# Attention block with a routed feed-forward on one core: the query projections of two heads over two halves of the rows, in seven products of summed blocks

## The chip, the cores and the metric

The kernel runs on one core of one Trainium2 chip. The metric is the device time of one launch in microseconds (us); less is better. A launch has five engines with a queue of their own each: TensorE (PE in the profile, and PEld for the loads of its stationary operand), VectorE (DVE), ScalarE (ACT), GpSimd (POOL) and SyncE (SP, which here only issues transfers). PSUM, into which TensorE writes, has eight banks of 512 numbers for each of its 128 partitions.

## What is computed

There are 8 sequences of 512 rows of 256 numbers, all in f32. The reference, cut to its core:

```python
def attn(x):                                   # b, t = 8, 512; 4 groups of 4 query heads, head size 128
    q = (x @ wq + bq).reshape(b, t, 4, 4, 128).transpose(0, 2, 3, 1, 4)
    k, v = halves of (x @ wkv + bkv) per group  # one key and one value head for each group
    q, k = q + pe, k + pe                      # pe: sinusoidal positions
    scores = where(causal, einsum("bgqtd,bgksd->bgqts", q, k) / sqrt(128), -inf)
    out = einsum("bgqts,bgksd->btgqd", softmax(scores), v)
    return out.reshape(b, t, 2048) @ wo

def ffn(h):                                    # 64 experts, 6 for each row, at most 64 rows for each expert
    probs = softmax(h @ gate_w.T); w, idx = top_k(probs, 6)
    y = sum over the 6 of w * down(silu(gate(h)) * up(h))    # rows beyond an expert's 64 are dropped
    return y + (silu(h @ sh_gate.T) * (h @ sh_up.T)) @ sh_down.T

x = x + layernorm(attn(layernorm(x)))
x = x + layernorm(ffn(layernorm(x)))
```

The change touches only `x @ wq + bq + pe`, for 22 of the 32 pairs of a sequence and a group of four query heads.

## The kernel before

The order of the work on every engine is written out by hand: inside `tc.manual_schedule` each engine runs its instructions in the order in which the code issues them. A main loop goes over 128 steps `k`. A step belongs to sequence `b = k // 16`, to place `s = k % 16` in it, to group `g = s // 4` and to part `m = k % 4` of the causal triangle; it handles four blocks of 32 rows for the four heads of its group. A step issues, in this order:

- `scores(k, q)` for q = 3, 2, 1, 0 (L404): one product of the 128 stacked queries with up to 512 keys into a bank of the pool `ps_s` (three banks). DVE then adds the mask and takes the minimum (L408, called the reduce here), and ACT takes the exponential and the row sum (L412). Between the first two and the last two of these, `turned(k - 1)` transposes the weights of the step before in blocks of 32 on DVE (L440), SP writes them to memory in four transfers to `ex_d` (L444) and reads them back as `et` (L450).
- `weigh(k)`: DVE takes the reciprocal of the sums (L418), and POOL multiplies the four blocks by it (L422, four instructions).
- `projections(k)` (L500): mostly four products of an attention output with `wo_sb` into the pool `ps_o`.
- `queries(k + 2)` (L360): the queries of two heads for one half of the rows of a sequence. The four blocks of 128 rows of a sequence, 0 to 3, make two halves, the inner one (1, 2) and the outer one (0, 3). The 256 numbers of a row lie in two chunks `c` of 128, so this is four products of 256 columns each, two chunks times two heads, into one bank; DVE then adds bias and positions, once for each head (L365, into tiles tagged `qt`).
- `mix(k - 2)` (L475): five products of values with `et` into `pav`; ACT adds the value bias (L486).
- `group_step(k)`: for m = 1 the keys of the next group (`keys`, L311, evicted by DVE at L313), for m = 2 and 3 half of its values (`values`, L322, evicted by ACT).

`pq` (queries), `pav`, `pk`, `pv` and most other results share the pool `ps_m` of three banks, used in turn. Pools `ps_s`, `ps_m` and `ps_o` fill all eight banks.

Between these parts `side(s, place)` issues the feed-forward of the sequence before (norms, the shared expert `shared`, the routing `route`, which ends in long chains on DVE), `ahead` prepares the next sequence (from s = 6: load, norm statistics on DVE at L80, `rs_a` on POOL at L90, normalising on DVE at L109, then at s = 9 and 10 the transposed rows `xnt`), and from step 94 on `routed` runs the 64 experts in 32 pairs, whose weights are loaded to tiles tagged `wgu` and `wd`. In the shared expert the gate product `psg` and the up product `psu` (L865) both lie in `ps_m` until DVE has combined them (L878, L879).

Of the kernel before, what the change touches and what calls it, by code (L numbers as in the profile page):

```python
# [11 lines left out]
F32 = mybir.dt.float32  # L12
# [28 lines left out]
ET_ROWS = EARLY * T  # L41
LROW = ROW + NX

@with_exitstack
def sandwich_kernel(ctx, tc, x, wq, bq_t, wkv, bk_t, bv, wo, gate_wt, w_gate, w_up, w_down,
# [7 lines left out]
    ps_s = ctx.enter_context(tc.tile_pool(name="ps_s", bufs=3, space=PSUM))  # L53
    ps_m = ctx.enter_context(tc.tile_pool(name="ps_m", bufs=3, space=PSUM))
    ps_o = ctx.enter_context(tc.tile_pool(name="ps_o", bufs=1, space=PSUM))
# [10 lines left out]
    lxg_d = dram.tile([NT - ET_ROWS, LROW], F32, tag="lxg_d", name="lxg_d")  # L66
    ly_d = dram.tile([NT - ET_ROWS, E], F32, tag="ly_d", name="ly_d")

    ident = const.tile([P, P], F32, tag="ident", name="ident")
# [78 lines left out]
    with ExitStack() as part:  # L148
# [158 lines left out]
        def keys(b, g):  # L307
            s = seqs[b]
            pk = ps_m.tile([P, T], F32, tag="m", name=f"pk_{b}_{g}")
            for c in range(NC):  # L310
                nc.tensor.matmul(pk, lhsT=wkv_sb[:, c, g, 0, :], rhs=s["xnt"][:, c, :], start=c == 0, stop=c == NC - 1)  # L311
            kt = s["kt"][g] = p2.tile([D, T], F32, tag="kt", name=f"kt_{b}_{g}")
            nc.vector.scalar_tensor_tensor(kt, pk, bk_sb[:, g : g + 1], pe_sb, ALU.add, ALU.add)  # L313

        def values(b, g, n):
            s = seqs[b]
            if n == 0:
                s["v"][g] = p2.tile([P, NI, D], F32, tag="v", name=f"v_{b}_{g}")
            pv = ps_m.tile([P, 2, D], F32, tag="m", name=f"pv_{b}_{g}_{n}")
            for i in range(2):  # L320
                for c in range(NC):
                    nc.tensor.matmul(pv[:, i, :], lhsT=s["xnt"][:, c, ts(2 * n + i, P)], rhs=wkv_sb[:, c, g, 1, :],  # L322
                                     start=c == 0, stop=c == NC - 1, skip_group_check=True)
            on_act(s["v"][g][:, ts(n, 2), :], pv)
# [24 lines left out]
        def queries(k):  # L349

            half, pair = divmod(k, 2)
            b, n = divmod(half, 2 * G)
            g, inner = divmod(n, 2)
            cols = slice(1, 3) if inner else slice(0, NI, 3)
            if not pair:
                halves[half] = p2.tile([D, 2 * NI, QPG, BS], F32, tag="qt", name=f"qt_{half}")
            pq = ps_m.tile([P, 2, 2, P], F32, tag="m", name=f"pq_{k}")
            for n in range(2):
                for c in range(NC):
                    nc.tensor.matmul(pq[:, n, :, :], lhsT=wq_sb[g][:, c, ts(2 * pair + n, D)],  # L360
                                     rhs=seqs[b]["xnt"][:, c, :].rearrange("p (u v) -> p u v", v=P)[:, cols, :],
                                     start=c == 0, stop=c == NC - 1, skip_group_check=True)
            for n in range(2):
                h = 2 * pair + n
                nc.vector.scalar_tensor_tensor(  # L365
                    halves[half][:, :, h, :].rearrange("d (u r) t -> d u r t", u=2),
                    pq[:, n, :, :].rearrange("d u (r t) -> d u r t", t=BS), bq_sb[:, g * QPG + h : g * QPG + h + 1],
                    pe_sb.rearrange("d (u r t) -> d u r t", u=NI, t=BS)[:, cols, :, :], ALU.add, ALU.add)

        by_rows = {}  # L370
# [97 lines left out]
        def mix(k):  # L468
            b, g, m, _ = units_of(k)
            et = live.pop(k)["et"]  # L470

            pav = ps_m.tile([P, QPG, 2, HALF], F32, tag="m", name=f"pav_{k}")
            for n, _, first, count in placed(k):
                for j in range(count):
                    nc.tensor.matmul(pav[:, :, n % 2, :], lhsT=seqs[b]["v"][g][:, j, :], rhs=et[:, :, first + j, :],  # L475
                                     start=j == 0, stop=j == count - 1, skip_group_check=True)
            if k % 2 == 0:
                results[k // 2] = {i: p2.tile([D, QPG, P], F32, tag="ao", name=f"ao_{k}_{i}", bufs=3)
                                   for i in tiles_at(k // 2)}
            bias = bv_sb[:, g : g + 1]  # L480
            for n, _, _, _ in placed(k):
                ao = results[k // 2][n // 2][:, :, ts(n % 2, HALF)]
                if k == NK - 1 and n < NI:
                    nc.vector.tensor_scalar_add(ao, pav[:, :, n % 2, :], bias)  # L484
                else:
                    nc.scalar.activation(ao, pav[:, :, n % 2, :], AF.Identity, bias=bias)  # L486
# [45 lines left out]
        def route(b, xg, l):  # L532

            lg = l.pop("lg")
            pg = ps_m.tile([P, NI, NX], F32, tag="m", name=f"pg_{b}")
            for i in range(NI):
# [25 lines left out]
            if b >= EARLY:  # L562

                yield
                pp = ps_m.tile([P, NI + 1, NX], F32, tag="m", name=f"pp_{b}")
                for i in range(NI + 1):
# [17 lines left out]

            pc = ps_m.tile([P, 2, P], F32, tag="m", name=f"pc_{b}")
            for j in range(NI):
# [12 lines left out]
        def tables():  # L599


            pm = ps_m.tile([NX, CAP], F32, tag="m", name="pm")
            nc.tensor.matmul(pm, lhsT=ident[:, NX:], rhs=keyed[0][:, :CAP], start=True, stop=True)
# [5 lines left out]
            for n, _ in enumerate(best(first, both)):  # L609
                if n % 2:  # L610
                    yield
            pk = ps_m.tile([P, NM], F32, tag="m", name="pslot")
            cols = ident[:NX, :NX].rearrange("p (m k) -> p k m", k=2)
# [12 lines left out]
        def free_slots():  # L626
# [10 lines left out]
            yield  # L637
            pf = ps_m.tile([P, 2, NX], F32, tag="m", name="pfree")
            nc.tensor.matmul(pf[:, 0, :], lhsT=onesf, rhs=both[:, CAP:], start=True, stop=True)
# [59 lines left out]
        def gate_up(key):  # L699
            l = pairs[key]  # L700
            pgu = ps_m.tile([P, 2, F], F32, tag="m", name=f"pgu_{key}")
            for c in range(2):
# [7 lines left out]
        def gate_up_hidden(key):  # L710
            l = pairs[key]
            pgu = l.pop("pgu")
            nc.vector.scalar_tensor_tensor(l["hid"], l["hid"], 1.0, pgu[:, 0, :], ALU.add, ALU.mult)
            nc.vector.scalar_tensor_tensor(l["hid"], l["hid"], 0.5, pgu[:, 1, :], ALU.mult, ALU.mult)
# [10 lines left out]
        def down(key):  # L725
            l = pairs[key]
            pd = ps_m.tile([P, E], F32, tag="m", name=f"pd_{key}")
            for c in range(2):
# [105 lines left out]

        def shared(b, xt2, l, banks="mmmmmm"):

            hid = p1.tile([P, len(SH_CHUNKS), T], F32, tag="hid", name=f"hid_{b}")
            banks, todo = iter(banks), {}

# [18 lines left out]
            for n, (f0, fw) in reversed(list(enumerate(SH_CHUNKS))):  # L858
                mw = min(P, fw + NX // 2)
                pgu = []  # L860
                for w_sb, name in ((sg_sb, "psg"), (su_sb, "psu")):
                    tag = next(banks)
                    pp = {"m": ps_m, "s": ps_s}[tag].tile([P, T], F32, tag=tag, name=f"{name}_{b}_{n}")
                    for c in range(NC):
# [11 lines left out]

                def hidden(n=n, fw=fw, gs=gs, pgu=pgu):
                    nc.vector.scalar_tensor_tensor(gs[:fw, :], gs[:fw, :], 1.0, pgu[0][:fw, :], ALU.add, ALU.mult)  # L878
# [17 lines left out]
            for n in range(2):  # L896
                py = ps_m.tile([P, 2, E], F32, tag="m", name=f"py_{b}_{n}")
                for k in range(2):
# [10 lines left out]
        def feed_forward(b):  # L909
# [50 lines left out]
            def shared_gate():  # L960
                l["f"] = shared(b, l["xt2"], l, "mmmmss" if b == B - 2 else "mmmmmm")
                next(l["f"])
# [183 lines left out]
        for k in range(NK):  # L1146
# [14 lines left out]
            scores(k, 1)  # L1161
            scores(k, 0)
            if k == NK - 1:
                projections(k)
# [4 lines left out]
            side(s, "A")  # L1169
            if k < NK - 1:  # L1170
                projections(k)
# [3 lines left out]
            if s == 9 and b <= EARLY + 1:  # L1175
                next(ahead)()
            if k + 2 < NK:
                queries(k + 2)
            if finishing:
                next(routed, None)  # L1180
            side(s, "M")
            if k >= 2:
                mix(k - 2)
            if b <= EARLY and s == 8:
                next(ahead)()
            if active and not finishing:
                next(routed, None)
            for _ in range((1, 1, 1, 1, 1, 1, 0, 0, 0, 0, 0, 0, 2, 2, 2, 2, 2, 2, 2, 1, 1, 1, 1)[k] if k < NH + 7 else 0):
                next(zeroing, None)
            if k == FIRST_FREE:  # L1190

# [36 lines left out]
        with tc.For_i(0, table["rest"], 1) as n:  # L1228
# [21 lines left out]
            for b in range(EARLY, B - 1):  # L1250
                y = p2.tile([P, NI, E], F32, tag="xnt", name=f"rest_y_{b}")
                nc.sync.dma_start(out=y, in_=rows_of(ly_d, b * T - ET_ROWS))
                for i in range(NI):
                    py = ps_m.tile([P, E], F32, tag="m", name=f"rest_py_{b}_{i}")
                    nc.tensor.matmul(py, lhsT=gts[b - EARLY][:, ts(i, P)], rhs=pairs["late"]["dd"], start=True, stop=True)
# [56 lines left out]
```

## Time and profile before

| | |
|---|---|
| time, median of 3 runs | 1380.87 us (1380.31 to 1383.84) |
| the profiled execution's own time | 1379.57 us |
| its span on the core | 1377.9 us |
| granted clock of TensorE | 0.997 |
| busy: PE / DVE / ACT / POOL | 1351.6 / 812.9 / 544.5 / 430.5 us |
| instructions on PE / DVE | 6354 / 2695 |

The profile is of one execution. "L360 PE MATMUL pq<-xnt,wq_sb 128x256" is a group of instructions: the line of the kernel, the engine, the operation, output<-inputs by tile name, and the shape of the output. An f32 product shows as two MATMUL instructions. Durations of neighbouring matmuls overlap in the record, so the time that a group takes on PE is read from where it starts to where the next group starts. In the timeline each line gives start, length, engine, line and tiles, and in brackets the idle time of that engine just before, with what released it.

### The profile page before, as it was taken

Reading aid. Unit: us, or ns where it says so; the run is one execution under the profiler, and the core shown is the slowest. Engines: PE = TensorE matmul, PEld = TensorE weight load, DVE = VectorE, ACT = ScalarE, POOL = GpSimd, SP = SyncE. Lnnn points to the kernel's source line nnn. Section 1 sums busy time; section 2 is a strip of 40 time slices with the busy share of each in tenths; the row PEclk is TensorE's granted clock in tenths of the full one; section 3 lists DMA queues with packets and bytes.
Section 4 is the critical chain, followed back from the end, with each engine's and each line's share of the span. In section 5 each row is a group of like instructions: output and inputs, shape, how many; then the busy total and the mean of one; then the engine's idle time right before and its main releaser. Section 6 shows DMA issues by size and latency. Waiting matters only on the chain. (4 is left out here: it accounts for less than half of the span.)

```text
span 1377.9 us, 20286 instructions
## 1 busy us (share of the span) xinstructions
PE 1351.6 (98%) x6354; PEld 1032.8 (75%) x6354; DVE 812.9 (59%) x2695; ACT 544.5 (40%) x1655; POOL 430.5 (31%) x732
## 2 busy tenths in 40 slices
PE   8999999999999999999999999999999999999997
PEld 6778887788778887788778876777666676777774
DVE  5565466655675466555765557566655545567555
ACT  3333344334443343334433443333443334435433
POOL 3222231213221232123221232124544454446521
PEclk9999999999999999999999999999999999999999
DMA  7666666555664566455664565459998889687712
GB/s 253 185 184 185 184 184 199 162 146 157 203 182 128 149 204 182 146 156 162 199 184 130 148 188 162 127 170 279 304 277 250 242 239 303 181 247 232 250 51 70
DMA packets 167386, 261.30 MB, mean 190 GB/s; under 512 B 17756, under 2 KB 141629, under 8 KB 167277
## 3 DMA queue, kind: packets, MB, share of 16 engines
q1 hardware_dynamic: 129389, 207.29, 50.8%
q10 hardware_dynamic: 31744, 43.26, 10.0%
q0 software_dynamic: 6144, 9.44, 3.4%
q8 instruction: 51, 0.84, 0.3%
q14 instruction: 58, 0.48, 0.1%
HBM read 147.99 MB, written 111.94 MB: 189 GB/s over the span
## 5 line engine op out<-in xcount | busy, mean ns | idle before, releaser
L422 POOL TENSOR_SCALAR e<-e,recip 128x512 f32<-128x512 f32 (+1 forms) x504 | 243.6, 521 | 727.0 <-DVE recip L418 632.7
L412 ACT ACTIVATE e<-e,least 128x32 f32<-128x32 f32 (+1 forms) x504 | 258.6, 514 | 257.4 <-DVE least L408 243.2
L475 PE MATMUL pav<-et,v 128*128 128x256 f32 x1280 | 298.3, 380 | 4.9 <-DMA et<-ex_d 4.8
L404 PE MATMUL psc<-kt,qt 128*128 128x32 f32 (+15 forms) x1024 | 277.3, 409 | 4.2 <-DVE least L408 3.1
L486 ACT ACTIVATE ao<-pav,bv_sb 128x256 f32<-128x256 f32 x255 | 107.2, 471 | 424.8 <-PE pav L475 404.1
L475 PEld LDWEIGHTS pav<-et,v 128*128 128x128 f32 x1280 | 242.9, 190 | 41.0 <-DMA et<-ex_d 4.9
L408 DVE CUSTOM_DVE_ANT_0 e<-psc,mask 128x32 f32<-128x32 f32 (+1 forms) x504 | 203.4, 429 | 102.1 <-PE psc L404 99.8
L500 PE MATMUL po<-wo_sb,ao 128*128 128x256 f32 x1024 | 242.2, 381 | 1.1 <-DVE ao L484 1.1
L360 PE MATMUL pq<-xnt,wq_sb 128*128 128x256 f32 x1024 | 242.0, 379 | 0.0
L500 PEld LDWEIGHTS po<-wo_sb,ao 128*128 128x128 f32 x1024 | 193.1, 190 | 57.8 <-issue 21.2
L360 PEld LDWEIGHTS pq<-xnt,wq_sb 128*128 128x128 f32 x1024 | 193.1, 190 | 27.6 <-issue 1.3
L404 PEld LDWEIGHTS psc<-kt,qt 128*128 128x128 f32 x1024 | 161.3, 191 | 65.3 <-DVE least L408 31.5
L440 DVE STREAM_TRANSPOSE eb<-e 128x1024 f32<-128x1024 f32 (+1 forms) x252 | 197.4, 821 | 1.9 <-POOL shift_y L806 1.1
L365 DVE SCALAR_TENSOR_TENSOR qt<-pq,bq_sb,pe_sb 128x256 f32<-128x256 f32 x256 | 111.4, 476 | 134.5 <-PE pq L360 134.5
L412 ACT ACTIVATION_READ_ACCUMULATOR e<-e,least 128x1 f32 x504 | 94.6, 188 | 0.0
L418 DVE RECIPROCAL recip<-total 128x4 f32<-128x4 f32 x128 | 22.8, 178 | 114.4 <-ACT e L412 113.0
L741 POOL DMA_INDIRECT y_d<-dd,idx x32 | 51.0, 1594 | 82.8 <-DMA y_d<-dd,idx 33.9
L322 PEld LDWEIGHTS pv<-wkv_sb,xnt 128*128 128x128 f32 x512 | 66.4, 192 | 4.2 <-issue 1.5
L322 PE MATMUL pv<-wkv_sb,xnt 128*128 128x128 f32 x512 | 67.7, 275 | 0.0
L311 PE MATMUL pk<-xnt,wkv_sb 128*128 128x512 f32 x128 | 61.2, 601 | 0.0
L313 DVE SCALAR_TENSOR_TENSOR kt<-pk,bk_sb,pe_sb 128x512 f32<-128x512 f32 x32 | 24.0, 750 | 56.8 <-PE pk L311 56.8
L115 DVE COPY ht<-pth 88x256 f32<-88x256 f32 x32 | 13.4, 418 | 64.2 <-PE pth L721 64.1
(212 smaller groups left out, 1119.5 us busy)
## 6 DMA issues: line engine op xcount, KB each, us to landing
ex_d<-eb SPq DMA_DIRECT2D x504, 160.0 KB
et<-ex_d SPq DMA_DIRECT2D x126, 640.0 KB
wgu<-in_w_gate ACTq DMA_DIRECT2D x32, 352.0 KB
wgu<-in_w_up ACTq DMA_DIRECT2D x32, 352.0 KB
wd<-in_w_down ACTq DMA_DIRECT2D x32, 352.0 KB
y<-y_d ACTq DMA_DIRECT2D x10, 512.0 KB
x<-in_x SPq DMA_DIRECT2D x7, 512.0 KB
out_dram<-x SPq DMA_DIRECT2D x7, 512.0 KB
```

The lines of the kernel that those rows point to most:

```text
L311: nc.tensor.matmul(pk, lhsT=wkv_sb[:, c, g, 0, :], rhs=s["xnt"][:, c, :], start=c == 0, stop=c == NC - 1)
L322: nc.tensor.matmul(pv[:, i, :], lhsT=s["xnt"][:, c, ts(2 * n + i, P)], rhs=wkv_sb[:, c, g, 1, :], start=c == 0, stop=c == NC - 1, skip_gro ...
L360: nc.tensor.matmul(pq[:, n, :, :], lhsT=wq_sb[g][:, c, ts(2 * pair + n, D)], rhs=seqs[b]["xnt"][:, c, :].rearrange("p (u v) -> p u v", v=P ...
L365: nc.vector.scalar_tensor_tensor(halves[half][:, :, h, :].rearrange("d (u r) t -> d u r t", u=2), pq[:, n, :, :].rearrange("d u (r t) -> d ...
L404: nc.tensor.matmul(psc[:, :w], lhsT=halves[k // 2][:, at, :, :].rearrange("d h t -> d (h t)"), rhs=seqs[b]["kt"][g][:, :w], start=True, st ...
L408: nc.vector.tensor_tensor_reduce(out=e, in0=psc[:, :w].rearrange("p (c t) -> p c t", t=BS), in1=mask[:, T - w :].rearrange("p (c t) -> p c ...
L412: nc.scalar.activation(e, e, AF.Exp, bias=l["least"][:, q : q + 1], scale=-1.0, accum_out=l["total"][:, q : q + 1])
L422: engine.tensor_scalar(e, e, recip[:, q : q + 1], 1.0, ALU.mult, ALU.mult)
L440: nc.vector.transpose(eb[:, :, first : first + count, :, :].rearrange("p a j r t -> p j a r t"), weighed[k % 2][:, end - count : end, :, : ...
L475: nc.tensor.matmul(pav[:, :, n % 2, :], lhsT=seqs[b]["v"][g][:, j, :], rhs=et[:, :, first + j, :], start=j == 0, stop=j == count - 1, skip ...
L486: nc.scalar.activation(ao, pav[:, :, n % 2, :], AF.Identity, bias=bias)
L500: nc.tensor.matmul(po[b][i // 2][:, i % 2, :], lhsT=ao[:, h, :], rhs=wo_sb[:, n // 2 * QPG + h, :], start=n == 0 and h == 0, stop=n // 2 = ...
```

## The change

For the groups 2 to 23 of the launch (counted over sequences: group index `4 * b + g`), the queries of two heads over both halves of the rows are formed together. Before, they are eight products of 128x128 weights with 256 columns of `xnt`: two heads, two halves, two chunks. Seen as a 2x2 block matrix of weights (head by chunk) times a 2x2 block matrix of rows (chunk by half), they are now seven products of blocks and of sums of blocks, in the form of Strassen's scheme with shared sums. The sums of weights (`join_heads`, once for each of the four groups) and of rows (`join_rows`, once for each of six sequences) are made on POOL. The seven products and the sums of their results are spread over three steps: `ask` and `ask_sum` in an even step, `answer`, `ask_rest` and `ask_fourth` in the next step, `answer_fourth` after the scores of the one after that. Groups 0, 1 and 24 to 31 keep `queries`.

One bank moves from `ps_m` (now two) to a new pool `ps_b`, which holds the products 4 to 7 (`back`); after the last such group the function `bank` hands it out in turn with the other two. The third product takes a bank of `ps_s`. In the shared expert of the first five sequences `psu` takes banks of `ps_s` instead of `ps_m`. In most even steps (`quiet`) `projections` and `ask` are issued before `weigh` instead of after it. The temporary tiles lie where the experts' tiles lie later.

```diff
+TH = T // 2
+JOINED_FROM, JOINED_TO = 2, (EARLY + 1) * G
-    ps_m = ctx.enter_context(tc.tile_pool(name="ps_m", bufs=3, space=PSUM))
+    ps_m = ctx.enter_context(tc.tile_pool(name="ps_m", bufs=2, space=PSUM))
+    ps_b = ctx.enter_context(tc.tile_pool(name="ps_b", bufs=1, space=PSUM))
+    banks = {"late": False, "kept": 0, "since": 0}
+    def bank(shape, name, kept=False):
+        banks["since"] += 1
+        if banks["late"] and not kept and banks["since"] > 2 - banks["kept"]:
+            banks["since"] = 0
+            return ps_b.tile(shape, F32, tag="b", name=name)
+        banks["kept"] += kept
+        return ps_m.tile(shape, F32, tag="m", name=name)
...
+        def join_heads(g):
+            t = p3.tile([P, 4, 2, D], F32, tag="wgu" if g >= 2 else "wd", name=f"heads_{g}")
+            w = wq_sb[g].rearrange("p c (n k d) -> p c k n d", k=2, d=D)
+            nc.gpsimd.tensor_add(t[:, 0], w[:, 0, 1], w[:, 1, 1])
+            nc.gpsimd.tensor_sub(t[:, 1], t[:, 0], w[:, 0, 0])
+            nc.gpsimd.tensor_sub(t[:, 2], w[:, 0, 0], w[:, 0, 1])
+            nc.gpsimd.tensor_sub(t[:, 3], w[:, 1, 0], t[:, 1])
+            joined[g] = t
+        def join_rows(b):
+            (x11, x12), (x21, x22) = [sides_of(seqs[b]["xnt"], c) for c in range(NC)]
...
+            nc.gpsimd.tensor_sub(t[:, 0], x12, x11)
+            nc.gpsimd.tensor_sub(t[:, 1], x22, t[:, 0])
+            nc.gpsimd.tensor_sub(t[:, 2], x22, x12)
+            nc.gpsimd.tensor_sub(t[:, 3], x21, t[:, 1])
+        def ask(k):
...
+            f = {1: (w[:, 0, 0, pair], x11), 2: (w[:, 1, 0, pair], x21), 3: (j[:, 3, pair], x22),
+                 4: (w[:, 1, 1, pair], t[:, 3]), 5: (j[:, 0, pair], t[:, 0]), 6: (j[:, 1, pair], t[:, 1]),
+                 7: (j[:, 2, pair], t[:, 2])}
...
+            front = bank([P, 2, 2, P], f"pq_front_{k}")
+            l["back"] = back = ps_b.tile([P, 2, 2, P], F32, tag="b", name=f"pq_back_{k}")
+            product(front[:, 0], f[1], first=True)
+            product(front[:, 1], f[2], last=True)
+            product(back[:, 0], f[6], first=True)
+            product(back[:, 1], f[7])
+            l["r"] = r = [p3.tile([D, 2, P], F32, tag=tag, name=f"{tag}_{k}") for tag in ("gxt", "ht")]
+            tiles = pe_sb.rearrange("d (u v) -> d u v", v=P)
+            nc.vector.tensor_add(r[0], front[:, 0], tiles[:, 1:3, :])
+            nc.vector.tensor_add(r[1], front[:, 0], tiles[:, 0:NI:3, :])
+            total(l, 0, 0, front[:, 1])
+        def total(l, n, u, bank_):
...
+            nc.vector.scalar_tensor_tensor(l["out"][n][u], blocks(bank_), l["bias"][n], blocks(l["r"][u]),
+                                           ALU.add, ALU.add)
+        def ask_sum(k):
+            nc.vector.tensor_add(l["r"][0], l["back"][:, 0], l["r"][0])
+        def answer(k):
+            product(l["back"][:, 0], l["f"][5])
+            nc.vector.tensor_add(l["r"][1], l["back"][:, 0], l["r"][1])
+            total(l, 1, 1, l["back"][:, 1])
+        def ask_rest(k):
+            third = ps_s.tile([P, 2, P], F32, tag="s", name=f"third_{k}")
+            product(third, l["f"][3], first=True, last=True)
+            total(l, 0, 1, third)
+        def ask_fourth(k):
+            product(l["back"][:, 1], l["f"][4], last=True)
+        def answer_fourth(k):
+            total(l, 1, 0, l["back"][:, 1])
...
-                l["f"] = shared(b, l["xt2"], l, "mmmmss" if b == B - 2 else "mmmmmm")
+                l["f"] = shared(b, l["xt2"], l, "mmmmss" if b == B - 2 else "msmsms" if b < EARLY else "mmmmmm")
...
             scores(k, 1)
             scores(k, 0)
+            if in_pairs(k - 1):
+                answer(k - 1)
+            if in_pairs(k - 2):
+                answer_fourth(k - 2)
+                banks["late"] = k // QPG + 1 == JOINED_TO
+            quiet = in_pairs(k) and not (1 <= b < EARLY and s in (10, 12))
+            if quiet:
+                projections(k)
+                ask(k)
...
             weigh(k)
...
-            if k < NK - 1:
+            if k < NK - 1 and not quiet:
                 projections(k)
...
-            if k + 2 < NK:
+            if k + 2 < JOINED_FROM * QPG or JOINED_TO * QPG <= k + 2 < NK:
                 queries(k + 2)
+            if in_pairs(k):
+                if not quiet:
+                    ask(k)
+                ask_sum(k)
+            if in_pairs(k - 1):
+                ask_rest(k - 1)
...
                 mix(k - 2)
+            if in_pairs(k - 1):
+                ask_fourth(k - 1)
...
+            if k in (0, 4, 7, 10):
+                join_heads({0: 2, 4: 3, 7: 0, 10: 1}[k])
+            if k == 0 or s == 11 and b < EARLY:
+                join_rows(b + 1 if k else 0)
```

`in_pairs(k)` holds for even k with `2 <= k // 4 + 1 < 24`, that is for the 44 even steps from 4 to 90. Every other `ps_m.tile` of the kernel becomes a call of `bank`.

## The prediction

> **What bounds the kernel now.** The page's first part and then the windows for steps 4 to 91, the steps that change (45.8 to 870.7 us):
>
> ```profile
> PE 1351.6 (98%) x6354; PEld 1032.8 (75%) x6354; DVE 812.9 (59%) x2695; ACT 544.5 (40%) x1655; POOL 430.5 (31%) x732
> ```
> ```profile
> core 0: us, PE busy (x) PEld busy (x) DVE busy (x) ACT busy (x) POOL busy (x), PEclk, DMA share, GB/s
> ...
> 45.80:870.70 824.90, 822.98 (x3699) 648.06 (x3699) 500.57 (x1630) 330.63 (x1039) 203.84 (x401) 1.00 0.59 171
> ```
>
> PE is busy for 822.98 of 824.90 us. The waits of PE in that window hold one entry, 1.9 us for DVE's reduces. So PE's own instructions set the pace, and a removed product is worth its full time as long as nothing makes PE wait. DVE is busy for 61% of this stage, so the question is its order, not its total.
>
> The price of a product, from PE's timeline in step 56: where the queries start and where the next group starts.
>
> ```profile
> 522.94 1.89 PE L360 MATMUL pq<-xnt,wq_sb 128*128 128x256 f32 x8
> 524.67 1.88 PE L865 MATMUL psg<-xt,sg_sb 128*128 128x512 f32 x4
> ```
>
> Four products take 524.67 - 522.94 = 1.73 us, 0.432 each (the 1.89 overlaps what follows).
>
> **What it removes.** 44 pairs (groups 2 to 23, two each) times one product of eight: 44 x 0.432 = 19.0 us of PE. The built program agrees in number: 308 products where 352 stood. The clock is 1.00 in the window, so there is nothing to win or lose there.
>
> **What it adds on DVE.** Eight operations of 128x256 for each pair instead of four. The old eviction (L365) is 0.88 us for two in the timeline, 0.43 each, mean 476 ns alone; another two-input operation of that size with one input in PSUM (L593) took 0.39. New ones are between 0.39 and 0.48; I take 0.43, the row of the same inputs. 176 more make 76 us, so (500.6 + 76) / (824.9 - 19) = 72% busy: not the bound by its sum. What decides is how they fall in a step. Step 54 is the busiest plain even step (DVE 6.91 of 8.49 us):
>
> ```profile
> 504.26 1.89 PE L500 MATMUL po<-wo_sb,ao 128*128 128x256 f32 x8
> 505.99 1.89 PE L360 MATMUL pq<-xnt,wq_sb 128*128 128x256 f32 x8
> ```
> ```profile
> 505.56 0.55 DVE L408 CUSTOM_DVE_ANT_0 e<-psc,mask 128x384 f32<-128x384 f32 x1
> 506.04 0.08 DVE L408 DVE_READ_ACCUMULATOR2_ANT least<- 128x1 f32 x1
> 506.99 0.18 DVE L418 RECIPROCAL recip<-total 128x4 f32<-128x4 f32 x1 [0.87 <-ACT e L412]
> ```
>
> After: the last sum of the pair before (answer_fourth) runs in DVE's 0.87 us of waiting, 506.12 to 506.55. PE does `po`, then `front` (0.87 us) until 506.86, then product 6 into the bank that answer_fourth has just read: 0.3 us to spare. In a step with m = 0, step 52, it is 0.6. DVE's evictions begin 0.2 us after a group ends (step 50: 475.66 to 475.86), so the three operations on `front` run from 507.06 to 508.35, and the reciprocal behind them at 508.4 instead of 506.99. Behind it wait POOL's weighing (1.89 us, to 510.3), then DVE's transposes of the next step, which began at 512.12: covered by 1.8 us, in step 52 by 0.6. If that cover were gone, the transfer of `et` would move by the difference. The value bank after it (`pv`) needs `front` evicted by 509.9, and it is at 508.4. In odd steps product 5 follows the scores and product 3 the projections; both come earlier than the old queries and DVE has one operation more, for which step 55 and its like have 4.2 us of idle and the shortest ones, s = 3, 1.4. Product 4 needs two sums that DVE made some 2 us before, at s = 3, where no projections lie ahead of it, 0.2 us before. So plain steps lose nothing.
>
> **Where it does cost.** Five places, each from the trace.
>
> (a) Step 0. POOL makes 8 sums there. One costs 0.695 (2.78 for four, L932):
>
> ```profile
> 492.01 2.78 POOL L932 TENSOR_TENSOR x<-x,o 128x256 f32<-128x256 f32 x4
> 42.72 2.40 PE L475 MATMUL pav<-et,v 128*128 128x256 f32 x10 [0.70 <-DMA et<-ex_d]
> ```
>
> They start when POOL is free at 25.3 and end at 30.9. The weighing of step 1, which began at 28.29, waits for them; its first two of four blocks are ready at 32.2, where DVE's transposes began at 31.13. They end 1.2 us later, and so does `et` for step 3, where PE already waited 0.70 us. Cost 1.2. The later sums (steps 4, 7, 10, then once in each sequence at s = 11) lie behind the weighing with 5 us free: nothing.
>
> (b) Step 8, sequence 0. The norm chain of the next sequence (statistics, `rs_a` on POOL, normalising) lies behind the reciprocal on DVE:
>
> ```profile
> 84.12 0.18 DVE L418 RECIPROCAL recip<-total 128x4 f32<-128x4 f32 x1 [0.95 <-ACT e L412]
> 87.37 1.38 DVE L109 TENSOR_SCALAR xn<-x,mv_a,rs_a 128x256 f32<-128x256 f32 x4 [0.49 <-POOL rs_a L90]
> 88.98 1.02 PE L404 MATMUL psc<-kt,qt 128*128 128x448 f32 x2 [0.32 <-DVE least L408]
> ```
>
> `front` ends at 84.33, the reciprocal comes at 85.9 instead of 84.12, 1.8 later, and the chain ends 1.8 later. PE waits 2.1 instead of 0.32. Cost 1.8.
>
> (c) s = 8 in sequences 1 to 4. The same chain ends in DVE's combining of `psg` and `psu`. There the chain had 1.3 us of waiting for ACT, so it ends about 0.5 later, at 531.45 in step 56. `psu` now lies in the bank that the second-last scores of step 57 need, at 530.8. Cost 0.65 x 4 = 2.6; bounds 0 and 1.
>
> (d) Steps 88 to 90. The chain of step 88 also carries the routing; it delays the scores already:
>
> ```profile
> 838.36 1.02 PE L404 MATMUL psc<-kt,qt 128*128 128x448 f32 x2 [1.60 <-DVE least L408]
> ```
>
> It comes 1.9 later. With two banks, `pav` follows two other products into the bank of `front` and waits for DVE: PE arrives at 833.2 and the bank is free at 833.5, and in step 90 at 855.8 and 856.2. Cost 1.9 + 0.3 + 0.4 = 2.6.
>
> (e) `pav` in odd steps starts 0.87 earlier (two products ahead of it instead of four). Step 69 had `et` issued at 645.53 and `pav` at 650.26, 4.73 us; in step 3, where PE waited, it was 38.45 to 42.72, 4.27. That leaves 0.46 of 0.87. Cost 0.4, in one or two steps.
>
> After step 92 the three banks rotate as before, save that a bank that is held is passed over. PE idles for 1.2, 1.8, 0.3 and 1.7 us in the four windows of 100 us from 900 to 1300: from a gain of 1 to a loss of 2; I take 0, since the same three banks serve the same instructions.
>
> Sum: 1.2 + 1.8 + 2.6 + 2.6 + 0.4 = 8.6 lost of 19.0, a net gain of 10.4. The profiled execution took 1379.57 around its span of 1377.9, so 1369.2 for that; the median of the runs is 1.3 higher, 1380.87, which gives 1370.5.
>
> One rule is weighed beside this. Two `xg` operations of L109 took 1.00 us beside POOL's weighing in step 54, 0.50 each, where four `xn` in step 8 took 1.38, 0.35 each: POOL costs DVE 0.15 there. The Trainium skill, SBUF — State Buffer, section "Who interferes with whom", says that a VectorE instruction with two SBUF inputs or in a two-port mode and a GpSimd instruction that reads SBUF shut each other out for a whole instruction. By the row, 40 sums cost DVE 6 us, spread over nine steps that have 2 to 4 us idle: nothing on PE. By the rule it could be 40 x 0.695 = 28 us by an estimate, 3.1 for each of those steps, and a few us of it would reach PE.
>
> **Rivals.** *The whole 19 us arrive.* The five places are short, and a stalled PE finds its next work ready, so DVE and `et` gain the time that PE lost. For it: PE idles in nothing but (b) and (d) now. Against it: (a), (b) and (d) are chains that are late already. Time 1362 to 1366.
>
> *More of the banks bite.* Two banks instead of three, with ACT's exponentials or the routing ahead of an eviction, cost another 0.1 us in each of the 88 steps, 9 us. For it: `pav`, `pk` and `pv` now wait for the allocation two before them. Against it: in plain steps the evictions are 1.5 us ahead or more. Time 1374 to 1379.
>
> *Slower: DVE holds product 6.* Place: the even step, where answer_fourth is read out between the last reduce and product 6, with 0.3 us to spare at m = 2 and 0.6 at m = 0. It decides once DVE is later than that; it eats the gain when the pairs lose (19.0 - 8.6) / 44 = 0.24 us each on average. With DVE 0.8 late (a slow start of the new operations, or reduces that drift), 22 steps lose 0.5 and 22 lose 0.2, 15.4 us: 1386. For it: one queue, no slack to speak of, and product 6 is behind every one. Against it: DVE has its 0.87 us of waiting for ACT exactly there, and the timeline is the same in every sequence.
>
> That it does not do what it says is excluded by the built order of instructions.
>
> **How the numbers follow.** Forecast (1366 to 1374): 0.50. Whole gain (below 1366): 0.17. Banks (1374 to 1379): 0.18. Slower (DVE on product 6): 0.10; the rest, 0.05, lies near no change. About 0.3% (4.1 us) can be told from no change, so faster means below 1376.7: 0.50 + 0.17 + most of the banks, 0.79; same 0.11; slower 0.10. The range from 1362 to 1379 leaves out the slower cases and a little below the whole gain. The forecast's own range is 1366 to 1374.
>
> **What would show it.** Right: PE's busy time some 19 us lower, its idle time about 8 higher, with DVE as the releaser of the scores of steps 9, 57 and 89, `et` at step 3, and no entry for product 6. The recurrent even step still takes 7.7 to 8.5 us, the odd step 0.43 less. Wrong: waits of product 6 or of `pav` in every step, a score's wait for the third product's bank, or POOL's weighing as the releaser of the transposes.

## The result and the profile after

The changed kernel takes 1373.15 us (median of 5 runs, 1372.25 to 1376.08) beside 1380.31 for the kernel before (1379.09 to 1383.84): a ratio of 0.9949, with a 95% interval from 0.9930 to 0.9967. That is faster, by 7.2 us where 10.4 were forecast. The profiled execution took 1376.08 around a span of 1374.4.

First the part of the profile with busy times, then the windows for steps 4 to 91 (45.29 to 861.65 us here), both of the changed kernel:

```profile
PE 1338.1 (97%) x6266; PEld 1017.6 (74%) x6266; DVE 874.6 (64%) x2871; ACT 543.9 (40%) x1655; POOL 458.3 (33%) x772
```
```profile
core 0: us, PE busy (x) PEld busy (x) DVE busy (x) ACT busy (x) POOL busy (x), PEclk, DMA share, GB/s
45.29:861.65 816.36, 810.02 (x3626) 635.33 (x3625) 562.91 (x1809) 330.11 (x1039) 226.17 (x433) 1.00 0.59 173
```

PE executes 88 instructions less, the two of each of 44 products. In these steps it idles for 6.3 us, where it idled for 1.9; 1.7 more follow at the start of step 92. DVE is busy for 69% of the stage (72% forecast).

Product 6 of step 54, from PE's timeline, and DVE beside it:

```profile
500.69 1.03 PE L418 MATMUL pq_front<-xnt,wq_sb 128*128 128x256 f32 x4
501.56 1.03 PE L418 MATMUL pq_back<-rows_joined,heads 128*128 128x256 f32 x4
```
```profile
500.74 0.48 DVE L453 SCALAR_TENSOR_TENSOR qt<-pq_back,bq_sb,gxt 128x256 f32<-128x256 f32 x1
501.75 0.42 DVE L444 TENSOR_TENSOR gxt<-pq_front,pe_sb 128x256 f32<-128x256 f32 x1 [0.54 <-PE pq_front L418]
```

The last sum ends at 501.22, 0.34 before product 6 begins, and PE waits for nothing. Step by step, from the scores of one step to those of the next: 40 of the 43 even steps from 6 to 90 are as long as before to 0.01 us, and 37 of the 43 odd steps are shorter by 0.43 to 0.49.

PE's wait for DVE's reduces in the kernel before, and then its waits in the changed kernel (releaser, total, times, longest; "..." stands for entries that are left out):

```profile
PE psc L404 <- DVE least L408: 3.1, 3, 1.6
```
```profile
PE psc L514 <- DVE least L518: 5.9, 3, 3.0
...
PE py L1006 <- DVE qt L453: 1.7, 1, 1.7
PE psc L514 <- DVE hid L993: 1.4, 4, 0.4
PE pgu L814 <- ACT dd L849: 1.1, 1, 1.1
...
PE pv L336 <- ACT ao L596: 0.7, 1, 0.7
PE pk L325 <- ACT ao L596: 0.7, 1, 0.7
...
PE pq L374 <- ACT dd L849: 0.4, 1, 0.4
```

The first entry, 3.1 us before, holds the scores of steps 9 (1.73) and 89 (2.99) and a wait of 1.18 late in the launch, which was there before; the third those of steps 25, 41, 57 and 73. There is none for product 6. The second and the last four had no counterpart: py in step 92, the others in steps 99 to 107, where the experts run. PE's timeline at py, and DVE's operation that it waits for:

```profile
865.65 1.56 PE L1006 MATMUL py<-sd_sb,hid 128*128 128x256 f32 x6 [1.72 <-DVE qt L453]
```
```profile
865.11 0.48 DVE L453 SCALAR_TENSOR_TENSOR qt<-pq_back,bq_sb,gxt 128x256 f32<-128x256 f32 x1
```

That is answer_fourth of step 90: py has been given the bank of `back`.

Counted from the scores of step 0, the changed kernel is 10.57 us ahead at the end of step 98; after step 124 only 3.5.

### The profile page after: what moved, and what is told of

It reads as the page before. It is cut to its first block, busy times and chain, and to the rows that moved or that the text cites. A ratio compares the mean times of both kernels' runs of the same rounds, so it can differ in the third digit from the quotient of the medians.

```text
span 1374.4 us, 20340 instructions
## 1 busy us (share of the span) xinstructions
PE 1338.1 (97%) x6266; PEld 1017.6 (74%) x6266; DVE 874.6 (64%) x2871; ACT 543.9 (40%) x1655; POOL 458.3 (33%) x772
## 5 line engine op out<-in xcount | busy, mean ns | idle before, releaser
L374 PE MATMUL pq<-xnt,wq_sb 128*128 128x256 f32 x320 | 75.8, 380 | 0.4 <-ACT dd L849 0.4
L418 PE MATMUL pq_back<-rows_joined,heads 128*128 128x256 f32 x264 | 71.8, 381 | 0.0
L374 PEld LDWEIGHTS pq<-xnt,wq_sb 128*128 128x128 f32 x320 | 59.3, 190 | 9.6 <-issue 1.3
L418 PEld LDWEIGHTS pq_back<-rows_joined,heads 128*128 128x128 f32 x264 | 50.5, 191 | 16.5 <-issue 8.5
L379 DVE SCALAR_TENSOR_TENSOR qt<-pq,bq_sb,pe_sb 128x256 f32<-128x256 f32 x80 | 34.9, 477 | 33.9 <-PE pq L374 31.2
```

The lines of the kernel that those rows point to most:

```text
L418: nc.tensor.matmul(out, lhsT=factor[0], rhs=factor[1], start=first, stop=last, skip_group_check=True)
```

## The experiments

Every four of the twelve kernels were timed beside the kernel before: 1378.25 us for the first four, 1379.09 and 1379.01 for the others. "More" or "less than the change" is against the change's 1372.34 of the first four, step by step against its profile there. The kernel before came out 0.8 us higher in the second and third four, so a difference taken across the sets is good to about 1 us.

**The changed kernel again.** No edit.

> The changed kernel once more, nothing edited. In its first profile steps 99 to 124 (the experts) took 7.05 us more than before, in six places where PE waits: pv 0.70, pk 0.70, pq 0.45, ptx 1.99, pgu 1.10, pav behind hid_late 0.84. Theory 1, these waits follow from the order of the instructions: they come back at the same steps, 4 to 7 us in all, and the time is 1372 to 1374. Theory 2, they belong to that one execution, which was also the slowest of its five runs: most are gone, and the profiled execution takes 1369 to 1371, near the forecast of 1370.5.

1372.34 us, ratio to before 0.9955 (0.9938 to 0.9971). At the end of step 98 it is 10.09 us ahead. Four losses come back to the hundredth: steps 99 (0.97), 101 (0.97), 104 (0.71) and 107 (1.32), 4.0 us. Those of steps 105 (1.99) and 124 (1.08) are gone. So both theories hold for a part: 4.0 us belong to the program, 3.1 to that execution (step 124 loses about 1 in some of the later profiles too).

**The count from 0 at step 92.**

```diff
-                banks["late"] = k // QPG + 1 == JOINED_TO
+                if k // QPG + 1 == JOINED_TO:
+                    banks |= {"late": True, "since": 0}
```

> The count of allocations starts at 0 when the third bank joins the other two, so that py_0 of step 92 does not get the bank that the fourth product still holds. Theory 1, the wait is due to that bank alone: PE's entry py <- DVE qt (1.72 us) is gone and the time falls by 1.7, to 1371.4. Theory 2, the time that PE gains is lost again in the experts' stage, whose waits are for transfers and other engines: the entry is gone and the time stays within 0.5 of 1373.2.

1371.42 us (0.9941, 0.9926 to 0.9956). The entry of py is gone and step 92 is 1.99 shorter than in the change, and in the profile nothing gives that back before step 124, which loses 1.07. By the medians the gain is 0.9, within the spread of the runs. So the bank was the cause of py's wait; how much of it reaches the end is not settled by this kernel alone.

**Banks strictly in turn.**

```diff
-        if banks["late"] and not kept and banks["since"] > 2 - banks["kept"]:
+        if banks["late"] and banks["since"] > 2:
```

with the edit before.

> After step 92 the three banks are handed out strictly in turn, as before the change; a bank that is held is not passed over. Theory 1, the waits of steps 99 to 124 come from the new order of banks: besides the 1.7 us of step 92, 3 to 5 us of pv, pk, pq, pgu and pav go, and the time is 1367 to 1369. Theory 2, they come from transfers and from the phase of ACT and DVE: only step 92 is gained, 1371 to 1372. Theory 3, passing over held banks was needed: pk, pv or pd now wait for psg and psu, and the time is 1374 or more.

1369.74 us (0.9936, 0.9920 to 0.9951), 2.6 less than the change. Beside step 92, steps 101 and 104 return to their old length (1.68), step 99 loses 0.35 more, and step 107 stays. Its waits:

```profile
PE pgu L814 <- ACT dd L849: 1.1, 1, 1.1
PE pv L336 <- DVE hid L825: 1.1, 1, 1.1
```

The waits for the banks of pk and pq go; pv, in another bank now, waits for the experts' hidden values instead. Passing over held banks is therefore one part, 1.3 of the 4.0; what remains depends on which bank meets which slow reader. Strict turn is not the old order either. This is pv of step 99 in the kernel before, with the last reads of the tiles just before it (pav) and three before it (pgu):

```profile
949.54 1.06 PE L322 MATMUL pv<-wkv_sb,xnt 128*128 128x128 f32 x8
```
```profile
949.52 0.84 ACT L486 ACTIVATE ao<-pav,bv_sb 128x256 f32<-128x256 f32 x2 [3.72 <-PE pav L475]
950.31 0.34 DVE L714 SCALAR_TENSOR_TENSOR hid<-hid,pgu 128x176 f32<-128x176 f32 x1
```

pv starts, without a wait, while both are still to be read. So it lies in the third bank, that of pq, which had been read by 948.3. The pool of before did not go strictly in turn there: it gave out the bank that was free. The change put pv behind the reader of pav (ao), this kernel behind that of pgu (hid).

**psg instead of psu in the score bank.**

```diff
-"msmsms" if b < EARLY
+"smsmsm" if b < EARLY
```

> In the shared expert of sequences 0 to 4 the gate product psg takes the score bank instead of the up product psu. DVE frees psg 0.69 us earlier than psu. Theory 1, the scores of steps 25, 41, 57 and 73 wait for the bank and nothing else (0.35 each): the four entries psc <- DVE hid go, 1.4 us, and with the rest of the 0.58 per step 1.4 to 2.3: the time is 1371 to 1371.8. Theory 2, psu in the pool of two banks now makes the queries or pav wait for DVE in the same steps: entries pq_front or pav <- DVE hid of 0.3 or more appear, and the time is 1373 or above.

1370.56 us (0.9938, 0.9923 to 0.9953), 1.8 less than the change. Steps 25, 41, 57 and 73 are each 0.58 shorter, now 0.43 below the kernel before, and the entry of hid is gone. Theory 1 holds. (Step 89 is 1.26 longer in its profile, by a second stretch of low clock; the last section comes to that.)

**The third product twice.**

```diff
-            product(third, l["f"][3], first=True, last=True)
+            for _ in range(2):
+                product(third, l["f"][3], first=True, last=True)
```

> The third product of every pair is issued twice into the same bank (the second writes the same numbers), 44 products more. Theory 1, PE is the bound in the odd steps and a product is worth its 0.432 us: every odd step of the 44 is 0.43 longer, 19.0 us in all, 1391.3. Theory 2, DVE or the transfers of et set the odd steps by now: the odd steps grow by clearly less, under 0.3, and the time is below 1386.

1390.99 us, 18.7 more than the change. 41 of the 44 odd steps are 0.43 or 0.44 longer. A product is worth its full time there: PE is still the bound.

**The read of the fourth product twice, and three times.**

```diff
-            total(l, 1, 0, l["back"][:, 1])
+            for _ in range(2):          # range(3) in the second kernel
+                total(l, 1, 0, l["back"][:, 1])
```

> The operation on DVE that reads the fourth product (answer_fourth) is issued twice, 0.48 us of DVE more between the last reduce and product 6. Theory 1, the slack of product 6 is 0.3 us at m = 2 and 0.6 at m = 0, as predicted: 22 steps lose 0.18 each, 4.0 us in all, the other 22 nothing, 1376.3. Theory 2, there was no slack and DVE already holds product 6: 44 steps lose 0.48, 21 us, 1393. Theory 3, the slack is 0.6 or more everywhere: nothing, 1372.3.

> The same operation three times, 0.96 us of DVE more. Theory 1, slack 0.3 and 0.6: 22 steps lose 0.66 and 22 lose 0.36, 22.4 us, 1394.8. Theory 2, no slack: 42 us, 1414. Theory 3, slack of 0.6 everywhere: 44 times 0.36, 15.8 us, 1388; of 1 us or more: 1372.3.

Twice: 1379.21 us (1375.96 to 1382.52), 6.9 more than the change. Twelve steps with m = 2 lose 0.34 each and those with m = 0 next to nothing, save step 52 (0.31). Step 92, where py waits for the same read, loses 0.52. The sum is 4.3 us up to step 125; the remaining 2.6 lie in the last steps, where et came late and the clock was low, and are not settled. Three times: 1391.46 us, 19.1 more. The same twelve steps lose 0.85 or 0.86, and 17 steps with m = 0 between 0.36 and 0.62. The entry that the rival asked for is there now:

```profile
PE pq_back L418 <- DVE qt L453: 11.2, 30, 0.6
```

Each repetition adds 0.52 us on DVE, so the slack is 0.52 - 0.34 = 0.18 us in steps with m = 2 and 1.04 - 0.47 = 0.57 with m = 0 (0.47 is the mean of the 17). The records had shown 0.34 in step 54, 0.16 more. Step 54 with three reads shows where that goes (DVE, PE's weight load, PE):

```profile
511.44 1.52 DVE L453 SCALAR_TENSOR_TENSOR qt<-pq_back,bq_sb,gxt 128x256 f32<-128x256 f32 x3
513.02 0.73 PEld L418 LDWEIGHTS pq_back<-rows_joined,heads 128*128 128x128 f32 x4 [1.00 <-DVE qt L453]
513.02 1.13 PE L418 MATMUL pq_back<-rows_joined,heads 128*128 128x256 f32 x4 [0.60 <-DVE qt L453]
...
513.99 1.24 PE L586 MATMUL pav<-et,v 128*128 128x256 f32 x5
```

The read ends at 512.96, and 0.06 later the first weight load and product 6 start together. In the change the load starts 0.22 before the product, beside the products on `front`. With the load waiting too, products 6 and 7 take 0.97 from their start to that of pav, 0.86 in the change (501.56 to 502.42). So 0.06 passes between the read and the product, and 0.11 is lost behind its start. The m = 2 steps with s = 2, and those with s = 10 in sequences 1 to 4, lose nothing even with three.

**Steps 8 and 88 in the old order.**

```diff
-quiet = in_pairs(k) and not (1 <= b < EARLY and s in (10, 12))
+quiet = in_pairs(k) and not (1 <= b < EARLY and s in (10, 12)) and k not in (8, 88)
```

> In steps 8 and 88 projections and ask are issued after weigh and after the norm chain, as in the kernel before, so that the chain on DVE does not lie behind the sums of front. Theory 1, the waits of steps 9 and 89 come from that order, and the granted clock of 0.50 to 0.67 after the wait of 2.99 us in step 89 from the length of the wait: step 9 falls by 1.4, step 89 by 1.4 and a further 1.65 of slow clock, 4.4 in all, 1368. Theory 2, the low clock has another cause and stays: 2.8 in all, 1369.6. Theory 3, front is now read behind the chain, and its bank holds up psg or pav by as much: 1372 or more.

1368.91 us (0.9932, 0.9915 to 0.9949), 3.4 less than the change. Step 9 is 1.22 shorter and step 89 4.40, but step 88 is 1.80 longer. PE's timeline there:

```profile
822.05 2.40 PE L585 MATMUL pav<-et,v 128*128 128x256 f32 x10 [1.64 <-issue]
...
825.87 1.02 PE L514 MATMUL psc<-kt,qt 128*128 128x448 f32 x2 [0.28 <-DVE least L518]
```

The order of DVE was the cause of both waits (theory 1), and the clock stays at 1.00 in step 89. Theory 3 also has its part: pav waits 1.64. The profile names no releaser; by the order of the two banks it takes that of the routing's pg, which ACT reads until about then (the last read starts at 821.81).

**The banks without the products.** `in_pairs` is false for every step, so that all pairs stay with `queries`; the sums on POOL are left out, and the third bank joins at step 92 with its count from 0.

> The banks of the change without its products: all pairs stay in the old queries, nothing is joined, ps_m has two banks until step 92 and the third joins then (with its count from 0), psu lies in a score bank. Nothing is gained, so the time is that of before (1378 to 1379 beside the other runs) plus what the banks cost. Theory 1, two banks are enough in plain steps, and the cost lies in the order of banks after step 92 (pv, pk, pq and pgu, 4.0 us in the profiles of the change): 4 us, 1382 to 1383. Theory 2, two banks cost 0.1 us in each of 88 steps: 9 us more, 1391. Theory 3, neither costs: 1379.

1384.48 us, slower than before by 5.5 (ratio 1.0041, 1.0027 to 1.0054). Plain steps are as long as before to 0.01 us, so two banks cost them nothing. Step 88 is 1.6 longer and step 89 as much shorter. Steps 25, 41, 57 and 73 lose 0.60 each, 2.4 us; steps 99, 101, 104 and 107 lose 0.97, 0.97, 0.72 and 1.32, the same 4.0 as in the change, by the same waits:

```profile
PE pgu L814 <- ACT dd L849: 1.1, 1, 1.1
...
PE pv L336 <- ACT ao L596: 0.7, 1, 0.7
PE pk L325 <- ACT ao L596: 0.7, 1, 0.7
...
PE pq L374 <- ACT dd L849: 0.5, 1, 0.5
```

Theory 1 holds for the experts' stage; that the score bank alone costs 2.4 was in none of the three.

**Three edits together** (turn, psg, steps 8 and 88), and the same with `projections` and `ask` of step 88 between the norm statistics and the routing:

> The three edits together: banks strictly in turn after step 92 (2.6 by the medians), psg instead of psu in the score bank (1.8), steps 8 and 88 in the old order (3.4). Theory 1, they lie in different steps and add up: 7.8 less than 1372.3, 1364.5. Theory 2, the transfers of et or the experts' stage take part of it back: 1367 or more.

> The three edits, and in step 88 projections and ask are issued behind the norm statistics but ahead of the routing's pg. With the old order pav of step 88 waited 1.64 us, because pg, which lay in its bank, was read by ACT only after DVE's maximum, and that lay behind the statistics; now pav takes the bank of front. Theory 1, pav waits 0.8 instead and DVE's chain ends as before: 0.8 less than the three edits, 1363.7. Theory 2, the routing's chain comes later by the operations on front, and step 89 takes the gain back: no difference.

The first takes 1364.61 us, a ratio to before of 0.9895 (0.9879 to 0.9910): 7.7 less than the change, where the single edits add up to 7.8. PE is busy for 1333.0 us in it, 18.6 below the kernel before. The second takes 1364.02 (0.9891, 0.9876 to 0.9906), no difference that can be told: in its profile pav still waits 1.5, step 88 is 0.33 shorter and step 89 0.14 longer. Both beat the two kernels of this case.

**A longer wait in the kernel before.**

```diff
+            if k == 88:
+                spare = p3.tile([D, 2, P], F32, tag="gxt", name="spare")
+                tiles = pe_sb.rearrange("d (u v) -> d u v", v=P)
+                for _ in range(3):
+                    nc.vector.tensor_add(spare, tiles[:, 1:3, :], tiles[:, 0:NI:3, :])
```

> The kernel before, with three additions of 128x256 on DVE behind the chain of step 88 and nothing else, so that PE's wait in step 89 grows from 1.60 to between 2.6 and 3.1 us. Theory 1, the granted clock falls because of the length of the wait: after it the rows show a clock of 0.50 to 0.7 for some us, and step 89 grows by 1.6 us more than the wait. Theory 2, the low clock in the changed kernel has to do with its instructions or its load, not with the wait: the clock stays at 1.00 and the step grows by the wait alone, 1.0 to 1.5.

In one profile the wait grew to 2.87 and step 89 by 1.26, with the clock at 1.00, as theory 2 expects (windows of that kernel; PEclk is the third number from the end):

```profile
837.00:839.00 2.00, 0.00 (x0) 0.00 (x0) 1.82 (x11) 0.00 (x0) 0.00 (x0) 1.00 0.00 0
839.00:841.00 2.00, 1.77 (x5) 0.92 (x6) 2.00 (x8) 0.85 (x4) 0.00 (x0) 1.00 0.00 0
841.00:843.00 2.00, 2.00 (x6) 0.90 (x5) 1.08 (x5) 1.61 (x5) 0.00 (x0) 1.00 0.58 132
```

The same place in the changed kernel, with a wait of 2.99:

```profile
826.00:828.00 2.00, 0.00 (x0) 0.00 (x0) 1.83 (x11) 0.00 (x0) 0.00 (x0) 1.00 0.00 0
828.00:830.00 2.00, 1.73 (x4) 0.99 (x5) 2.00 (x8) 0.85 (x4) 0.00 (x0) 0.67 0.00 0
830.00:832.00 2.00, 2.00 (x4) 0.99 (x3) 1.91 (x7) 1.39 (x4) 0.00 (x0) 0.50 0.57 131
```

So theory 1 falls in this form: the length of a wait alone does not decide. But the change's instructions are not needed either: the kernel before has a stretch at 0.50 as well, at 1306.8 us of its profile. What goes with it is told in the last section. The kernel's time in this one run, 1382.5, is not read further.

Up to step 88 this kernel is the one before, so it also shows a second execution of that. The writes of step 2 and the read of `et` in step 3 show it, in the first profile of the kernel before and then here (SP's issues):

```profile
32.72 2.27 SPq L444 DMA_DIRECT2D ex_d<-eb  x4
38.45 0.34 SPq L450 DMA_DIRECT2D et<-ex_d  x1
```
```profile
33.36 2.23 SPq L444 DMA_DIRECT2D ex_d<-eb  x4
38.08 0.34 SPq L450 DMA_DIRECT2D et<-ex_d  x1
```

From the last issue of a write to the read it took 3.46 us there and 2.49 here, and here PE does not wait in step 3. Steps 1 to 3 take 22.34 and 21.27 us together.

## Why the prediction was right, and where its terms were not

The sign and the range were right, and so was the main mechanism. Its terms in turn, by the first profile unless another is named:

- **The products.** 44 times 0.43: right. Doubling one of them cost 18.7. PE's busy time fell by 13.5 in the change's first profile, where steps 89 and 105 ran in part at half clock, and by 18.6 with the three edits, where no step up to 125 did.
- **Plain steps lose nothing.** Right. The slack of product 6 was put at 0.3 and 0.6; it measures 0.18 and 0.57. The first omits the 0.06 between DVE's end and PE's start and the 0.11 of a weight load that is no longer covered. The slower rival was close: one more operation of DVE starts it, two cost as much as the products bring.
- **(a) Step 0.** Cost 1.2 forecast; beside the first profile none shows, steps 1 to 3 are together 0.43 shorter. But that profile of before is the odd one: its 3.46 us from the last write to the read of et stand beside 2.49 in the other execution of the same steps, 2.40 with the banks alone, and 2.1 to 2.3 in all eleven kernels with the sums. The wait of 0.70 from which the term starts belonged to that one execution. POOL's sums end at 30.9, as worked out, and DVE's transposes wait 0.73 us for the weighing behind them. Beside the banks alone, whose steps 1 to 3 take 21.31 us, the eleven take 21.73 to 21.98: the sums cost 0.4 to 0.7. So the chain was right and its cost about twice too large.
- **(b) Step 8.** The wait of step 9 grew by 1.41 (1.8 forecast), and the old order of step 8 took 1.22 off again.
- **(c) s = 8.** 0.58 in each of four steps, 2.3 in all (2.6 forecast). The size was right and its reason only in part: without any product the score bank costs 0.60 as well, so the bank is the cause, not the later chain.
- **(d) Steps 88 to 90.** 3.4 instead of 2.6. The wait grew by 1.39 (1.9 forecast) and the two others came to 0.3 (0.7), but the clock behind the wait cost 1.7 that the sum did not have.
- **(e) pav in odd steps.** 0.4 forecast; none in the first profile, 0.79 in step 37 of the second and none there in the others.
- **Step 92.** Not in the sum. Without queries it should have been 1.73 shorter; py took the bank that DVE had still to read, and it was 0.27 longer: 2.0.
- **After step 92.** Taken as 0, between a gain of 1 and a loss of 2; it is a loss of 4.0 in both profiles of the change. This is the step that failed: "the same three banks serve the same instructions" overlooked that a bank is not free with its turn but with its reader. The pool of before gave pv of step 99 the bank that was free; the new rule put it behind ao, and strict turn behind hid. Passing over held banks accounts for 1.3 of the 4.0, and the rest was not won back by any kernel here.

Up to step 98 the errors cancel. Beside the first profile (a), (b), (c) and (e) were together 2.7 too high, (d)'s waits 0.9, and the clock and step 92, 3.7 together, were missing. That the 10.57 there is so near the forecast of 10.4 is luck, and 1.1 of it is the slow start of that profile of before. Behind step 98 the experts' stage loses 4.0: 10.57 - 1.1 - 4.0 leaves 5.5, where the medians show 7.2, or 5.9 beside the second set of runs of before.

The rival that the banks bite had the right size for a wrong place: 0.1 in each step was excluded by the kernel with the banks alone, where the banks cost 6.4 us in eight steps and next to nothing elsewhere (its first steps are 1.0 shorter than in the odd profile of before). On the rule of ports weighed in the prediction (the Trainium skill, SBUF — State Buffer, "Who interferes with whom"): steps with POOL's sums, such as steps 11 and 27, kept their gain of 0.43 in full, so nothing of it reached PE here. The row that stood against the rule was read as an average: of the two xg operations of step 54 only the second ran beside the weighing, and it took 0.68 us where the first took 0.41, so a hit costs 0.27 and not 0.15.

## What to carry to other kernels

When a kernel is bound by one engine, price a removed instruction in full, and then look for the places where its successors are already late: they took two thirds of it here, in a dozen of 128 steps, and moving two of them back was worth as much as 8 products. A pool that is split and later joined again needs its turn worked out tile by tile, by the reader that frees each bank: neither a rule that passes over held banks nor strict turn was the old order here. Slack read between two records is too large by what a late start costs beside the wait, here 0.06 us until the product starts and 0.11 of a weight load that no longer runs ahead.

## What the runs showed of the hardware

The granted clock of TensorE is recorded in stretches of 3.41 us or whole multiples, the last one of a launch apart. A stretch that began at full clock was followed by half clock (0.50) whenever PE had been idle for 1.96 us or more of it: 17 of 17 in the 14 traces of this case, behind the first 30 us and ahead of the last stretches, in which PE has no work left. With 1.89 to 1.94 it was one of four, with 1.84 or less none. Behind a stretch at half clock less was enough for another: it came in three of three with 0.84 to 1.49 us of idle time, and in none with 0.52 or less. With psg in the score bank that was the case in step 89. A wait that crosses from one stretch into the next counts in two parts: the 2.87 us above fell into 0.95 and 1.92 and left the clock alone, a wait of 3.22 near the end of the same execution fell into 1.6 and 1.6 and did too, and in the first profile of the change a wait of 1.99, 1.89 of it in one stretch, lowered it: step 105 took 1.99 more there, 1.55 of waiting being usual. One stretch at half clock costs PE up to half of it, 1.7 us, as it did in step 89. The Trainium skill, TensorE: Matmul & The Clock Gate, "Part 1: The HAM clock gate", has the free-running window of this length and says that half clock follows an idle window of about 3.4 us; the traces agree on the window, and show that a little over half of it idle is enough.

So the price of a wait of PE is not its length alone: one of 2 to 3 us costs itself, or itself and 1.7, and once itself and about 3 (step 89 with psg in the score bank), by where it lies among stretches that the program does not set: the first boundary lies 4.9 to 7.9 us after the start in the 14 traces. That is part of the spread between executions of the same kernel.
